# A graph layer on one core: the places of four pairs in one copy, a row of places in PSUM, two more gather buffers and narrower last blocks

## The chip, the core and the metric

The kernel runs on one core of a Trainium2 chip. A core has a matrix engine (PE, TensorE, with its weight loads counted apart as PEld), a vector engine (DVE), a scalar engine (ACT), a general engine (POOL, GpSimd), which here does nothing but gather rows by index, and SyncE (SP), which issues the plain copies from and to device memory. Working data lie in SBUF (128 partitions); PE writes to PSUM, eight banks of 512 f32 columns per partition. Each engine takes its instructions in order, and semaphores tie the engines together.

The metric is the device time of one launch in microseconds (us). The kernel before took 3597.59 us, the median of three runs from 3594.44 to 3604.85.

## What is computed

A message-passing layer over 12,500 nodes and 400,000 edges, with a GRU at the nodes. Edges come sorted by `dst`.

```
h   = max(layernorm(x), 0)
m   = relu(concat(h[src], h[dst], ea) @ w1 + b1) @ w2 + b2      # per edge, ea has 32 features
agg = segment_sum(m, dst)
gi, gh = agg @ w_ih + b_ih, h @ w_hh + b_hh
r, z = sigmoid(i_r + h_r), sigmoid(i_z + h_z);  n = tanh(i_n + r * h_n)
out = x + (1 - z) * n + z * h
```

## The kernel before

**Preparation.** The nodes are normalised in batches; `hT_all` keeps h transposed in SBUF, and the table A = h @ w1[0:128] goes to device memory. Then small tables are made on DVE (lines 349 to 391): the first node of each pair (`base_f`), per block its first node (`blk_f`), the offsets of its pairs (`off_f`, `off_i`) and the step from the block before (`step_f`, `step_i`).

**The loop over edges.** 128 edges make a tile, 8 tiles a *pair* k (391 of them), half a pair a *unit* u (782). In one pair all edges go to two windows of 32 nodes each, since `dst` is sorted. Per pair:

- `gather` (line 136): eight indirect copies on POOL bring the rows A[src] of 128 edges each into a G buffer (a few first pairs take x instead). G buffers come from a pool of `GBUFS` and, at first, another of `EARLY`.
- `fetch_d` (486) and `fetch` (478): on SP's queue the places (`dst`, broadcast to 32 partitions, one copy for each half, into a tile Ld) and the edge features (into partitions 64 to 95 of a tile L), for QP = 2 pairs at a time.
- `onehot_T` (496): DVE compares Ld with the node numbers and writes the transposed one-hots into partitions 0 to 63 of L.
- `window_copy`, `window_product`, `window_rows` (506, 522, 529): the 64 columns of h of the two windows times w1[128:256], written with the bias into RW.
- `pre` (593): PE multiplies L with RW, which adds the window's row and the feature part. `add` (616): DVE adds G. `relu` (628): ACT writes RB.
- `onehot` (537): DVE compares each edge's place in its window (`dloc`, f16) with the row 0 to 31 (`iota`, f16 in SBUF). `seg` (636): PE sums RB over the edges of a window into a PSUM bank; `take` (649) copies the sums out.

`stages(u)` runs these as a pipeline: one-hots three pairs ahead, `pre` three units ahead, `add` and `relu` two units ahead, `seg` of the unit itself.

**By hand.** 43 of the 391 pairs are not gathered by POOL: their columns of h are copied one at a time, by ACT (line 789, 19 pairs) and DVE (796 and 801, 24 pairs), spread over the loop from u = 2 * JOBS0 on, where JOBS0 = 2 * EARLY + GBUFS.

**The nodes.** Every 14 pairs make a block of 512 nodes. `node(b)` (657) is a generator: it adds up the pairs' sums (PE, lines 674 to 682), carries the overlap of the block before (`carry`), makes four gates (`gate`, each of products with `brow`, `whh_s`, `w2ih`), the elementwise work and the transposes back, and stores. The loop runs one step of it per unit, in phase 3 of `other`. The last block (13 pairs) runs as a whole behind the loop.

PSUM holds two banks each for `oh` (window products, and the transposes of the preparation), `pre` and `seg`, and one each for `nd` and `misc`. `check_windows` sets a flag when the windows don't hold all edges, and a slow general path would follow; for these inputs it isn't taken.

Of the kernel before, what the change touches and what calls it, by code (L numbers as in the profile page):

```python
# [28 lines left out]
V = 32  # L29
# [4 lines left out]
NB = -(-NP // BP)  # L34
DMIN = 320
QP = 2
# [5 lines left out]
GBUFS = 7  # L42
# [13 lines left out]
def tile_gnn(ctx: ExitStack, tc: tile.TileContext, x, src, srcT, dstT, dstP, eaT, eaP, w1, b1, w2T, b2,  # L56
# [12 lines left out]
    ps1 = ctx.enter_context(tc.tile_pool(name="ps1", bufs=1, space=bass.MemoryType.PSUM))  # L69
    dram = ctx.enter_context(tc.tile_pool(name="dram", bufs=1, space=bass.MemoryType.DRAM))  # L70
# [138 lines left out]
    with tc.tile_pool(name="pp", bufs=3) as pp:  # L209
# [76 lines left out]
        for q in range(NC + 3):  # L286
            if q < NC:
                b, i0, c, e, P, n0 = chunk(q)
                if c == 0:
                    stat(b + 2)  # L290
                    fin(b + 1)
            if 1 <= q <= NC:
                b, i0, c, e, P, n0 = chunk(q - 1)
                pts[q - 1] = ps2.tile([128, 512], F32, name="oh")
# [40 lines left out]

    p3 = ctx.enter_context(tc.tile_pool(name="p3", bufs=3, reuse_waits="tile"))
# [31 lines left out]
    nc.vector.tensor_scalar(blk_f, base_f[:, ::BP], float(N - BW), None, op0=ALU.min)  # L368
# [8 lines left out]
    for k0, k1, b0, b1_, n in ((0, (NB - 1) * BP, 0, NB - 1, BP),  # L377
                               ((NB - 1) * BP, NP, NB - 1, NB, NP - (NB - 1) * BP)):
        nc.vector.tensor_tensor(
            off_f[:, b0:b1_, :n], base_f[:, k0:k1].rearrange("o (b n) -> o b n", n=n),  # L380
            blk_f[:, b0:b1_, None].to_broadcast([1, b1_ - b0, n]), op=ALU.subtract)
        nc.vector.tensor_copy(base_i[:, b0:b1_, :n],
                              base_f[:, k0:k1].rearrange("o (b n) -> o b n", n=n))
    nc.vector.tensor_scalar(off_i, off_f, float(BW - V - SHIFT), 0.0, op0=ALU.min, op1=ALU.max)
# [3 lines left out]
    step_c = const.tile([1, NB], F32, name="step_c")  # L388
    nc.vector.tensor_scalar(step_c, step_f, float(BW), float(DMIN), op0=ALU.min, op1=ALU.max)
# [60 lines left out]
    def check_windows():  # L450
# [8 lines left out]
        pm = ps2.tile([128, 512], F32, name="oh")  # L459
# [3 lines left out]
        nc.vector.tensor_reduce(f[:, 6:7], off_f, AX.XY, ALU.max)  # L463
        nc.vector.tensor_reduce(f[:, 7:8], off_f, AX.XY, ALU.min)
        nc.vector.tensor_scalar(f[:, 1:2], f[:, 6:7], float(BW - V - SHIFT), None, op0=ALU.is_gt)
        nc.vector.tensor_scalar(f[:, 5:6], f[:, 7:8], 0.0, None, op0=ALU.is_lt)
        nc.vector.tensor_reduce(f[:, 2:3], step_f, AX.X, ALU.max)
        nc.vector.tensor_scalar(f[:, 3:4], blk_f[:, NB - 1:NB], float(N - BW), None,
                                op0=ALU.not_equal)
        nc.vector.tensor_copy(f[:, 4:5], f[:, 5:6])  # L470
        nc.vector.tensor_reduce(f[:, 6:7], f[:, 0:6], AX.X, ALU.max)
# [3 lines left out]
    Ls, Ds, OH, RT, HE, SEG = ({} for _ in range(6))  # L475
# [10 lines left out]
    def fetch_d(q):  # L486
        if q * QP >= NP:
            return
        n = min(QP, NP - q * QP)
        c = slice(q * QP * 512, (q * QP + n) * 512)  # L490
        Ds[q] = p3.tile([2 * V, QP * 512], I32, name="Ld")
        for a in range(2):
            nc.sync.dma_start(Ds[q][V * a:V * (a + 1), :n * 512],
                              dstP[a:a + 1, c].to_broadcast([V, n * 512]))

    def onehot_T(k):
        if k >= NP:
            return
        c = slice((k % QP) * 512, (k % QP + 1) * 512)
        nc.vector.tensor_scalar(Ls[k // QP][:2 * V, c], Ds[k // QP][:, c], node_of[:, k:k + 1],  # L500
                                None, op0=ALU.is_equal)
# [3 lines left out]

    def window_copy(k):
        if k >= NP:
            return
        b = k // BP
        if k % BP == 0:  # L510
            n = min(BP, NP - k)
# [25 lines left out]
    def onehot(k):  # L537
# [3 lines left out]
        OH[k] = OHB[k % len(OHB)]  # L541
        for a in range(2) if k == 0 else (None,):
            if a is None:
# [3 lines left out]
                i = iota[:, None, None, :]  # L547
            else:
# [3 lines left out]
                i = iota[:, None, :]  # L552
# [96 lines left out]
    def take(k):  # L649
        if k < 0:  # L650
            return
        pm = SEG.pop(k)
        nc.vector.tensor_copy(sums[:, k % BP, :], pm[:2 * V, :D])  # L653
        nc.scalar.copy(dcol[:2 * V, NP - 1 - k:NP - k], pm[:2 * V, D:D + 1])  # L654


    def node(b):

        def carry(o, p, d):
            m = BW - DMIN  # L660
# [4 lines left out]
        g0 = nc.sync.value_load(blk_i[0:1, b:b + 1], min_val=0, max_val=N - BW)  # L665
        xb = p3.tile([128, 4, D], F32, name="xb", bufs=1)
        nc.sync.dma_start(xb, x[bass.ds(g0, BW), :].rearrange("(p i) f -> p i f", i=4))
        n = min(BP, NP - b * BP)
        _, offs = nc.values_load_multi_w_load_instructions(
            off_i[0:1, b, 0:n], engines=[ET.PE], min_val=0, max_val=BW - V - SHIFT,  # L670
            skip_runtime_bounds_check_because="clamped above")
        pt = ps1.tile([128, 512], F32, name="nd")
        pd = ps1.tile([128, 512], F32, name="misc")
        nc.tensor.matmul(pt, zrow[:, :128], zrow, start=True, stop=False)
# [3 lines left out]
        nc.tensor.matmul(pd, zrow[:, :128], zrow, start=True, stop=False)  # L678
        for i in range(n):
            c = NP - 1 - (b * BP + i)  # L680
            nc.tensor.matmul(pd[:, bass.ds(offs[i], V + SHIFT)], dcol[:, c:c + 128], spot_h,
                             start=False, stop=i == n - 1)
        d = nc.vector.value_load(step_i[0:1, b:b + 1], min_val=DMIN, max_val=BW)
# [4 lines left out]
        g = nc.tensor.value_load(blk_i[0:1, b:b + 1], min_val=0, max_val=N - BW)  # L688
        hT = hT_all[:, bass.ds(g, BW)]

        def gate(name, i, with_h, with_s):
            c = slice(i * D, (i + 1) * D)
            ci = slice(2 * D, 3 * D) if i == 3 else c
            pg = ps1.tile([128, 512], F32, name=name)
            nc.tensor.matmul(pg, brow[:, c], DEG[:, :BW], start=True, stop=False)  # L695
            if with_h:
                nc.tensor.matmul(pg, whh_s[:, ci], hT, start=False, stop=not with_s)  # L697
            if with_s:
                nc.tensor.matmul(pg, w2ih[:, ci], TOT[:, :BW], start=False, stop=True)  # L699
            return pg  # L700

        def temp():
            return p3.tile([128, BW], F32, name="gt", bufs=3)
# [18 lines left out]
        gv = nc.vector.value_load(blk_i[0:1, b:b + 1], min_val=0, max_val=N - BW)  # L722
        q = r
        nc.vector.tensor_tensor(q, hT_all[:, bass.ds(gv, BW)], t, op=ALU.subtract)
# [5 lines left out]
        po = ps1.tile([128, 512], F32, name="nd")  # L730
# [5 lines left out]
        nc.sync.dma_start(out[bass.ds(g0, BW), :].rearrange("(p i) f -> p i f", i=4), xb)  # L736
# [109 lines left out]
    for q in range(2):  # L846
        fetch_d(q)
        fetch(q)
    fetch_d(2)
# [38 lines left out]

    for u in range(NU):
        k, h = divmod(u, 2)  # L890
        gathers(u)
        if h == 0:
            if k % QP == 0:
                fetch_d(k // QP + 3)
                fetch(k // QP + 2)
            if k % BP == 0 and k:
                nodes_left.append([node(k // BP - 1), 2])
# [12 lines left out]
        def other(phase):  # L910
# [9 lines left out]
            if phase == 3:  # L920
# [183 lines left out]
```

## Time and profile before

| | before |
|---|---|
| median of three runs | 3597.59 us (3594.44 to 3604.85) |
| the profiled execution: its time / its span | 3598.83 us / 3597.1 us |
| busy: PE, DVE, ACT, POOL | 74%, 68%, 70%, 75% of the span |
| mean granted TensorE clock | 0.778 |
| gathers on POOL: count, mean | 2704 from A at 969 ns, 77 from x at 948 ns |
| copies on SP's queue for dst / for features | 392 / 196 |

A row of the page's groups reads: line, engine, operation, tile written <- tiles read, shapes, count | busy us, mean ns of one | idle time of the engine just ahead of them, and what ended most of it. "issue" there is idle time in which the engine waited for nothing that the profile shows. Rows of waits read: engine, tile and line that waited <- who ended the wait: us in total, times, longest. Rows of the timeline and of the chain begin with the start in us from the span's start and the length in us. The span is the time from the first to the last instruction; a run's time lies a little above it.

### The profile page before, as it was taken

What the parts mean: (1) busy time and instruction counts of PE and PEld (TensorE: products, weight loads), DVE (VectorE), ACT (ScalarE), POOL (GpSimd) and SP (SyncE); (2) the same over time, 40 slices, a digit from 0 to 9 for tenths busy, and PEclk for the clock granted to TensorE, in tenths of its full rate; (3) what the DMA queues carried; (4) which work ended last, traced back from release to release, by engine and by line L of the source; (5) the groups of instructions that cost most, each with busy time, mean ns of one, the idle gap of its engine ahead of it and who ended that gap; (6) DMA issues with size and microseconds to landing.
All of it is one profiled execution on the core that took longest, in us unless ns stands there. A gap on an engine that the chain in (4) does not pass through costs nothing. (4 is left out here: it accounts for less than half of the span.)

```text
span 3597.1 us, 76803 instructions
## 1 busy us (share of the span) xinstructions
PE 2664.4 (74%) x13674; PEld 1618.5 (45%) x13674; DVE 2445.7 (68%) x16547; ACT 2506.7 (70%) x20936; POOL 2694.2 (75%) x2789
## 2 busy tenths in 40 slices
PE   7697677677767776876777777677767776776876
PEld 6454344444434443443444444444444443443443
DVE  8766667677667667667666677676667677766652
ACT  5445567777777777777777777777777677767771
POOL 7677777777777777777777777777777777777774
PEclk9787888787877877777786888787777778786777
DMA  6333333333333333333333333333333333333331
GB/s 207 86 100 87 86 88 88 92 86 89 87 88 85 87 89 85 89 86 89 86 86 89 86 88 88 92 87 88 88 87 86 85 89 84 89 85 87 81 86 41
DMA packets 145458, 321.60 MB, mean 89 GB/s; under 512 B 58913, under 2 KB 64844, under 8 KB 144967
## 3 DMA queue, kind: packets, MB, share of 16 engines
q0 software_dynamic: 88992, 182.43, 20.7%
q1 hardware_dynamic: 55831, 134.16, 13.5%
q14 instruction: 379, 3.10, 0.3%
q8 instruction: 112, 1.84, 0.2%
q10 hardware_dynamic: 144, 0.07, 0.0%
HBM read 302.60 MB, written 13.84 MB: 88 GB/s over the span
## 5 line engine op out<-in xcount | busy, mean ns | idle before, releaser
L145 POOL DMA_INDIRECT G<-A,src_i x2704 | 2620.3, 969 | 835.3 <-issue 780.1
L789 ACT COPY HE_act<-hT_all 128x4 uint8 x19456 | 1983.0, 189 | 585.6 <-issue 583.7
L796 DVE SCALAR_TENSOR_TENSOR both<-hT_all 128x4 uint16 x12288 | 1097.0, 155 | 954.0 <-issue 947.2
L601 PE MATMUL pre<-RW,L 128*128 128x256 f32 x3128 | 1171.0, 503 | 730.5 <-DVE G L626 633.8
L601 PEld LDWEIGHTS pre<-RW,L 128*128 128x128 f32 x3128 | 677.1, 241 | 1068.8 <-DVE G L626 811.0
L632 ACT ACTIVATE RB<-G 128x512 f32<-128x512 f32 x676 | 424.5, 628 | 353.5 <-issue 143.4
L645 PE MATMUL seg<-RB,OH 128*32 128x129 f32 x6250 | 642.8, 340 | 4.3 <-ACT dcol L654 4.3
L626 DVE TENSOR_TENSOR G<-pre,G 128x512 f32<-128x512 f32 x676 | 462.5, 684 | 64.1 <-DMA G<-A,src_i 41.7
L645 PEld LDWEIGHTS seg<-RB,OH 128*32 128x32 f32 x6250 | 349.5, 130 | 232.2 <-issue 127.9
L526 PE MATMUL oh<-w1b,hw 128*64 128x128 f32 x782 | 213.0, 364 | 123.8 <-DVE hw L519 120.4
L535 DVE TENSOR_TENSOR RW<-oh,b1b 32x128 f32<-32x128 f32 x782 | 217.2, 278 | 11.5 <-PE oh L526 6.2
L526 PEld LDWEIGHTS oh<-w1b,hw 128*64 128x64 f32 x782 | 91.6, 166 | 294.2 <-DVE hw L519 210.6
L500 DVE TENSOR_SCALAR L<-Ld,node_of 64x512 f32<-64x512 int32 x391 | 192.2, 492 | 0.7 <-issue 0.6
L553 DVE TENSOR_TENSOR OH<-dloc,iota 128x256 f32<-128x256 f16 (+1 forms) x392 | 161.0, 411 | 0.2
L676 PE MATMUL nd<-spot,sums 64*128 64x40 f32 x782 | 116.9, 319 | 0.0
L676 PEld LDWEIGHTS nd<-spot,sums 64*128 64x128 f32 x782 | 113.0, 229 | 7.9 <-issue 7.9
L653 DVE COPY sums<-seg 64x128 f32<-64x128 f32 x391 | 107.1, 274 | 4.9 <-PE seg L645 3.7
L640 PE MATMUL seg<-zrow 1*64 1x129 bf16 x391 | 106.4, 272 | 3.0 <-ACT dcol L654 3.0
L519 DVE COPY hw<-hT_all 128x64 f32 x391 | 87.6, 224 | 24.6 <-issue 23.4
L801 DVE COPY HE_dve<-both 128x512 uint8<-128x512 uint8 x192 | 88.0, 458 | 6.6
L145 POOL DMA_INDIRECT G<-in_x,src_i x77 | 73.0, 948 | 25.1 <-issue 22.9
L640 PEld LDWEIGHTS <-zrow 1*64 1x64 bf16 x391 | 43.4, 111 | 94.7 <-issue 94.7
(148 smaller groups left out, 1605.0 us busy)
## 6 DMA issues: line engine op xcount, KB each, us to landing
Ld<-in_dstP SPq DMA_DIRECT2D x390, 128.0 KB
L<-in_eaP SPq DMA_DIRECT2D x195, 256.0 KB
G<-A,src_i POOLq DMA_INDIRECT x2704
xb<-in_x SPq DMA_DIRECT2D x28, 256.0 KB
out<-xb SPq DMA_DIRECT2D x28, 256.0 KB
xs<-in_x SPq DMA_DIRECT2D x11, 512.0 KB
A<-asb SPq DMA_DIRECT2D x11, 512.0 KB
src_i<-in_srcT SPq DMA_DIRECT2D x19, 80.0 KB
```

The costliest lines, as they stand in the source:

```text
L145: nc.gpsimd.indirect_dma_start(out=G[k][:, j, a, :], out_offset=None, in_=table, in_offset=bass.IndirectOffsetOnAxis(ap=src_i[c][:, i:i + ...
L500: nc.vector.tensor_scalar(Ls[k // QP][:2 * V, c], Ds[k // QP][:, c], node_of[:, k:k + 1], None, op0=ALU.is_equal)
L526: nc.tensor.matmul(PB_[k][:2 * V, :D], HW.pop(k).rearrange("p a v -> p (a v)"), w1b, start=True, stop=True)
L535: nc.vector.tensor_tensor(RW[k % 4][s, a, :], pm[s, :D], b1b[s, :], op=ALU.add)
L553: nc.vector.tensor_tensor(o, d.to_broadcast(shape), i.to_broadcast(shape), op=ALU.is_equal)
L601: nc.tensor.matmul(PP[u][:, 2 * i:2 * i + 2, :], Ls[k // QP][:, c0:c0 + 128], RW[k % 4], start=True, stop=not raw)
L626: nc.vector.tensor_tensor(RT[u], PP.pop(u), RT[u], op=ALU.add)
L632: nc.scalar.activation(o[:, :, :D], RT.pop(u), AF.Relu)
L645: nc.tensor.matmul(SEG[k][V * a:V * (a + 1), :D + 1], OH[k][:, j, a, :], RB[u % 3][:, (j % 2) * 2 + a, :D + 1], start=False, stop=all(b != ...
L676: nc.tensor.matmul(pt[:, bass.ds(offs[i], V + SHIFT)], sums[:, i, :], spot, start=False, stop=i == n - 1)
L789: nc.scalar.copy(he[:, e * 4:e * 4 + 4], column(v))
L796: nc.vector.scalar_tensor_tensor(both[:, (e0 % PIECE + i) // 2, :], column(vals[i + 1]), 256.0, column(vals[i]), op0=ALU.mult, op1=ALU.add)
```

## The change

The change does these things at once:

- **Copies.** QP goes from 2 to 4, Ld and `fetch_d` go. One copy brings the places of both halves of four pairs, broadcast to 64 partitions, straight into partitions 0 to 63 of L, and a second the features. `onehot_T` works in place. L has 2 buffers in place of 3. The copies of a group are issued where the last pair of the group two before it begins (k % 4 == 3).
- **Row of places.** The two `oh` banks become two fixed tiles `wide`; columns 128 to 159 of each hold a copy of `iota` as f32, and `onehot` reads it from the bank that the next window product doesn't write.
- **G buffers.** GBUFS goes from 7 to 9; JOBS0, and with it the start of the columns by hand, moves from 15 to 17 pairs.
- **Blocks.** `BLOCKS` lists the blocks: 26 of 14 pairs and 512 nodes as before, then 12 pairs (512 nodes), 7 (320), 6 (256) and 2 (128). The tables are made in five groups. `node` works on the block's width. A node starts behind `take` in phase 3; from pair 376 on it runs two steps a unit, from pair 389 on four.

```diff
+BLOCKS = [(BP * b, BP, BW) for b in range(26)] + [(364, 12, BW), (376, 7, 320), (383, 6, 256), (389, 2, 128)]
+NB = len(BLOCKS)
+NW = 27
+LEAST = [DMIN] * (NW + 1) + [192, 128]
+QP = 4
-GBUFS = 7
+GBUFS = 9
...
+    wide = [ps1.tile([128, 512], F32, name=f"wide{i}") for i in range(2)]
...
+    for w in wide:
+        nc.vector.tensor_copy(w[:, D:D + V], iota)
...
+    groups = [(0, NW - 1, 0, BP, BW)] + [(b, b + 1) + BLOCKS[b] for b in range(NW - 1, NB)]
+    for b0, b1_, k0, n, w in groups:
+        nc.vector.tensor_scalar(blk_f[:, b0:b1_], base_f[:, k0:k0 + (b1_ - b0 - 1) * n + 1:n], float(N - w),
+                                None, op0=ALU.min)
...
+    for b0, b1_, k0, n, w in groups:
+        ks = base_f[:, k0:k0 + (b1_ - b0) * n].rearrange("o (b n) -> o b n", n=n)
+        nc.vector.tensor_tensor(off_f[:, b0:b1_, :n], ks,
+                                blk_f[:, b0:b1_, None].to_broadcast([1, b1_ - b0, n]), op=ALU.subtract)
+        nc.vector.tensor_copy(base_i[:, b0:b1_, :n], ks)
+        nc.vector.tensor_scalar(off_c[:, b0:b1_, :n], off_f[:, b0:b1_, :n], float(w - V - SHIFT), 0.0,
+                                op0=ALU.min, op1=ALU.max)
+        nc.vector.tensor_scalar(step_c[:, b0:b1_], step_f[:, b0:b1_], float(BLOCKS[max(b0 - 1, 0)][2]),
+                                float(LEAST[b0]), op0=ALU.min, op1=ALU.max)
...
-        Ls[q] = p3.tile([128, QP * 512], F32, name="L")
+        Ls[q] = p3.tile([128, QP * 512], F32, name="L", bufs=2)
+        p = dstP[:, c]
+        nc.sync.dma_start(
+            Ls[q].bitcast(I32)[:2 * V, :n * 512],
+            bass.AP(tensor=p.tensor, offset=p.offset, ap=[list(p.ap[0]), [0, V], [1, n * 512]]))
         nc.sync.dma_start(Ls[q][2 * V:, :n * 512], eaP[:, c])
...
-        nc.vector.tensor_scalar(Ls[k // QP][:2 * V, c], Ds[k // QP][:, c], node_of[:, k:k + 1],
-                                None, op0=ALU.is_equal)
+        nc.vector.tensor_scalar(Ls[k // QP][:2 * V, c], Ls[k // QP].bitcast(I32)[:2 * V, c],
+                                node_of[:, k:k + 1], None, op0=ALU.is_equal)
...
-        PB_[k] = ps2.tile([128, 512], F32, name="oh")
+        PB_[k] = wide[k % 2]
...
+        row = wide[(k + 1) % 2][:, D:D + V]
...
-                i = iota[:, None, None, :]
+                i = row[:, None, None, :]
...
+            m = before - LEAST[b]
             nc.vector.tensor_tensor(o[:, 0:m], p[:, 0:m], o[:, bass.ds(d, m)] if b else
                                     o[:, BW:BW + m], op=ALU.add)
-            nc.vector.tensor_copy(o[:, m:BW], p[:, m:BW])
+            if m < w:
+                nc.vector.tensor_copy(o[:, m:w], p[:, m:w])
+            if w < before:
+                nc.vector.memset(o[:, w:before], 0.0)
...
+    def steps(k, phase):
+        hurry = 1 if k < BLOCKS[NW][0] else 2 if k < BLOCKS[-1][0] else 4
+        return phase >= 4 - hurry
...
-            if k % QP == 0:
-                fetch_d(k // QP + 3)
+            if k % QP == QP - 1:
                 fetch(k // QP + 2)
-            if k % BP == 0 and k:
-                nodes_left.append([node(k // BP - 1), 2])
...
-            if phase == 3:
+                if k and k == BLOCKS[block(k)][0]:
+                    for it, _ in nodes_left:
+                        run(it)
+                    nodes_left[:] = [[node(block(k) - 1), 1 if k > BLOCKS[NW][0] else 2]]
+            for _ in range(steps(k, phase)):
                 step(nodes_left)
```

In `check_windows` the two long reductions of `off_f` and three small operations become one reduction of the marks that the tables now hold.

More of the change, by code (lines that the diff above doesn't have):

```diff
@@ L376, in tile_gnn @@
     nc.vector.memset(off_f, 0.0)
[L377 to L384, printed above, removed]
+    off_c = const.tile([1, NB, 16], F32, name="off_c")
+    nc.vector.memset(off_c, 0.0)
+    step_c = const.tile([1, NB], F32, name="step_c")
     nc.vector.tensor_tensor(step_f[:, 1:], blk_f[:, 1:], blk_f[:, :-1], op=ALU.subtract)
     nc.vector.memset(step_f[:, 0:1], float(BW))
-    step_c = const.tile([1, NB], F32, name="step_c")
-    nc.vector.tensor_scalar(step_c, step_f, float(BW), float(DMIN), op0=ALU.min, op1=ALU.max)
+    for b0, b1_, k0, n, w in groups:
[7 more added lines that the diff above has]
+                                float(LEAST[b0]), op0=ALU.min, op1=ALU.max)
+    nc.vector.tensor_copy(off_i, off_c)
+    nc.vector.tensor_tensor(off_f, off_f, off_c, op=ALU.not_equal)
     nc.vector.tensor_copy(step_i, step_c)
@@ L462, in check_windows @@
         nc.vector.tensor_reduce(f[:, 0:1], pm[0:1, :128], AX.X, ALU.max)
[L463 to L466, printed above, removed]
+        nc.vector.tensor_reduce(f[:, 1:2], off_f, AX.XY, ALU.max)
         nc.vector.tensor_reduce(f[:, 2:3], step_f, AX.X, ALU.max)
-        nc.vector.tensor_scalar(f[:, 3:4], blk_f[:, NB - 1:NB], float(N - BW), None,
+        nc.vector.tensor_scalar(f[:, 3:4], blk_f[:, NB - 1:NB], float(N - BLOCKS[-1][2]), None,
                                 op0=ALU.not_equal)
-        nc.vector.tensor_copy(f[:, 4:5], f[:, 5:6])
-        nc.vector.tensor_reduce(f[:, 6:7], f[:, 0:6], AX.X, ALU.max)
+        nc.vector.tensor_reduce(f[:, 6:7], f[:, 0:4], AX.X, ALU.max)
         nc.vector.tensor_copy(flag, f[:, 6:7])
-    Ls, Ds, OH, RT, HE, SEG = ({} for _ in range(6))
+    Ls, OH, RT, HE, SEG = ({} for _ in range(5))
     hand = {}
@@ L551, in onehot @@
                 shape = [128, e - a * GRP, V]
-                i = iota[:, None, :]
+                i = row[:, None, :]
             nc.vector.tensor_tensor(o, d.to_broadcast(shape), i.to_broadcast(shape),
@@ L677, in node @@
                              start=False, stop=i == n - 1)
-        nc.tensor.matmul(pd, zrow[:, :128], zrow, start=True, stop=False)
+        nc.tensor.matmul(pd, zrow[:, :128], zrow[:, :w], start=True, stop=False)
         for i in range(n):
-            c = NP - 1 - (b * BP + i)
+            c = NP - 1 - (k0 + i)
             nc.tensor.matmul(pd[:, bass.ds(offs[i], V + SHIFT)], dcol[:, c:c + 128], spot_h,
                              start=False, stop=i == n - 1)
-        d = nc.vector.value_load(step_i[0:1, b:b + 1], min_val=DMIN, max_val=BW)
+        d = nc.vector.value_load(step_i[0:1, b:b + 1], min_val=LEAST[b], max_val=before)
         yield 1
@@ L693, in gate @@
             ci = slice(2 * D, 3 * D) if i == 3 else c
-            pg = ps1.tile([128, 512], F32, name=name)
-            nc.tensor.matmul(pg, brow[:, c], DEG[:, :BW], start=True, stop=False)
+            pg = ps1.tile([128, 512], F32, name=name)[:, :w]
+            nc.tensor.matmul(pg, brow[:, c], DEG[:, :w], start=True, stop=False)
             if with_h:
@@ L698, in gate @@
             if with_s:
-                nc.tensor.matmul(pg, w2ih[:, ci], TOT[:, :BW], start=False, stop=True)
+                nc.tensor.matmul(pg, w2ih[:, ci], TOT[:, :w], start=False, stop=True)
             return pg
         def temp():
-            return p3.tile([128, BW], F32, name="gt", bufs=3)
+            return p3.tile([128, BW], F32, name="gt", bufs=3)[:, :w]
         pr = gate("nd", 0, True, True)
@@ L729, in node @@
         yield 1
-        po = ps1.tile([128, 512], F32, name="nd")
+        po = ps1.tile([128, 512], F32, name="nd")[:w // 4, :]
         for i in range(4):
@@ L846, in tile_gnn @@
     for q in range(2):
-        fetch_d(q)
         fetch(q)
-    fetch_d(2)
     for k in range(3):
```

54 lines of the change are left out of this document (22 added, 32 removed).

## The prediction

> **What bounds the kernel now.** I read the page first, then the waits of POOL, the waits of DVE by stretches, and last the end of the run.
>
> ```profile
> span 3597.1 us, 76803 instructions
> PE 2664.4 (74%) x13674; PEld 1618.5 (45%) x13674; DVE 2445.7 (68%) x16547; ACT 2506.7 (70%) x20936; POOL 2694.2 (75%) x2789
> L145 POOL DMA_INDIRECT G<-A,src_i x2704 | 2620.3, 969 | 835.3 <-issue 780.1
> ...
> POOL G L145 <- issue: 803.0, 2635, 0.3
> ...
> POOL G L145 <- PE misc L586: 11.6, 1, 11.6
> ...
> L145 POOL DMA_INDIRECT G<-A,src_i x2704: 940/944/2132, 99.9 to 3554.4; - x194
> ```
>
> No engine is over 75% busy, yet POOL never rests: between two gathers lie 0.3 us of issue, and only once in the whole run, for 11.6 us, does it wait for anybody. From 99.9 to 3554.4 us it issues 2704 gathers, (3554.4 - 99.9 - 11.6) / 2703 = 1.274 us apart. A gather takes 944 ns at the median, 969 on the mean: 2704 x 25 ns = 68 us are delays.
>
> ```profile
> DVE both L796 <- issue: 622.5, 515, 2.5
> DVE hw L519 <- issue: 14.5, 18, 1.1
> ...
> L553 DVE TENSOR_TENSOR OH<-dloc,iota 128x256 f32<-128x256 f16 x240 | 98.8, 412 | 0.0
> ...
> DVE G L626 <- DMA G<-A,src_i: 14.5, 13, 2.4
> ...
> DVE G L626 <- DMA G<-A,src_i: 22.9, 6, 4.3
> ...
> DVE G L626 <- DMA G<-A,src_i: 4.2, 1, 4.2
> ```
>
> These are DVE's waits from 264 to 2400 us (first two rows, with L553 of the same stretch), from 2400 to 3400, from 3400 to 3557 and behind. Up to 2400 DVE waits for nothing but its own register loads: it is full, at 2136 / 240 = 8.9 us a pair, 4.45 us a unit. From 2400 on it catches up with POOL and waits 14.5 us for gathers; at the very end 22.9 + 4.2 = 27.1 us more. So two engines are at parity: POOL made faster by itself gives DVE back 14.5 + 27.1 = 41.6 us and not one more.
>
> ```profile
> 3485.00:3513.00 28.00, 26.70 (x150) 15.74 (x150) 14.66 (x37) 23.46 (x204) 21.44 (x22) 1.00 0.32 84
> 3513.00:3526.00 13.00, 13.00 (x101) 8.73 (x95) 6.75 (x18) 4.39 (x13) 9.95 (x11) 1.00 0.37 102
> 3526.00:3557.00 31.00, 13.52 (x84) 7.95 (x82) 6.56 (x16) 3.91 (x9) 22.34 (x24) 0.86 0.21 54
> ...
> 3557.00:3597.10 40.10, 29.05 (x73) 12.94 (x73) 6.97 (x13) 2.65 (x6) 0.00 (x0) 0.50 0.02 8
> ...
> 3557.11 0.70 DVE G L626
> ...
> 3560.42 5.70 PE nd L676 x26
> ...
> 3568.25 2.04 PE nd L695 x2
> ...
> 3587.77 0.61 ACT gt L720
> ...
> 3591.03 0.69 DVE xb L734
> ```
>
> The windows show length, then busy time of PE, its loads, DVE, ACT, POOL, and the granted clock. The hand-made columns end here, and PE is full (26.7 of 28 us, then 13.0 of 13.0) at clock 1.00. Then everything waits for gathers, PE falls to 13.5 of 31 us, and the tail behind the last add (3557.11 to 3597.1, 40 us) runs at a granted 0.50. The chain of waits names its parts: sums of 13 pairs 5.7 us, gates 19.5 us (3568.25 to 3587.77).
>
> **The parts: more G buffers, 7 to 9.** Pair 11 now waits 11.6 us for the buffer of pair 0. With two more buffers pairs 11 and 12 (16 gathers, 20 us) are gathered meanwhile, so the wait goes whole: POOL -11.6 us.
>
> **The row of places in PSUM.**
>
> ```profile
> 1011.15 0.42 DVE L553 TENSOR_TENSOR OH<-dloc,iota 128x256 f32<-128x256 f16 x1
> 1011.20 1.19 POOL L145 DMA_INDIRECT G<-A,src_i  x1 [0.30 <-issue]
> ...
> 1026.40 0.69 DVE L626 TENSOR_TENSOR G<-pre,G 128x512 f32<-128x512 f32 x1
> 1026.43 0.95 POOL L145 DMA_INDIRECT G<-A,src_i  x1 [0.30 <-issue]
> ...
> L712 DVE TENSOR_TENSOR gt<-gt,misc 128x512 f32<-128x512 f32 x28 | 19.2, 687 | 14.6 <-PE misc L697 11.1 <-ACT gt L708 2.8
> L726 DVE TENSOR_TENSOR gt<-gt 128x512 f32<-128x512 f32 x28 | 19.0, 680 | 4.3 <-ACT gt L720 4.3
> ```
>
> L553 reads two SBUF tensors; the gather started inside it takes 1.19 us instead of 0.944, that is, something it needs 0.12 us after its start waits until 1011.57, where L553 ends. L626 reads one tensor from PSUM and one from SBUF, covers that same moment, and the gather takes 0.95. The change makes L553 of L626's kind. A one-hot of 412 ns meets that moment in 412 / 1274 of the cases and then delays by 206 ns: 391 x 0.0666 = 26 us of POOL's 68. I take -26 (bounds 0 and -26). On DVE the operand costs what L712 against L726 costs, 7 ns, 391 times 0 to 3 us: 0.
>
> [...]
>
> **One copy for the places of 4 pairs, one-hots in place.** 588 issues on SP become 196. SP is a bystander:
>
> ```profile
> SPq L493 <- DVE L L500: 2920.5, 191, 25.2
> q1 hardware_dynamic: 55831, 134.16, 13.5%
> q0 software_dynamic: 88992, 182.43, 20.7%
> ...
> 205.26 0.69 DVE L626 TENSOR_TENSOR G<-pre,G 128x512 f32<-128x512 f32 x1 [0.37 <-PE pre L601]
> ...
> 209.04 0.69 DVE L626 TENSOR_TENSOR G<-pre,G 128x512 f32<-128x512 f32 x1 [0.37 <-PE pre L601]
> ```
>
> It waits 2920 us for buffers, so fewer issues cost and give 0. The bytes stay the same. What changes is the time allowed: the L tile of a group comes free with the last product of the group two before, and its first one-hot stands 6 units later, 26.7 us at 4.45 us a unit. Queue q1 keeps 16 rings busy 13.5% of the span, 7770 us for 134.16 MB, so 17.3 GB/s a ring: 512 KB take 1.9 us on sixteen rings. The new pattern has the two rows of dstP outermost; if that leaves it two rings, 15.2 us, and 15.2 / (1 - 0.207) = 19.2 beside the gathers. Both fit in 26.7. They don't fit where units are short: around pairs 16 to 23, without jobs, two units take 3.78 us (205.26 to 209.04), six 11.3. Two groups there wait 2 x 0 to 2 x 8 us; I take 5, since the pattern speaks for two rings.
>
> **The prologue and the flags.**
>
> ```profile
> 99.79 0.84 DVE L365 TENSOR_SCALAR node_of<-base_b,place_c 32x391 f32<-32x391 f32 x2 [13.13 <-POOL place_c L360]
> ...
> 101.26 0.43 DVE L376 MEMSET off_f<- 1x448 f32 x1
> ...
> 102.65 0.15 DVE L379 TENSOR_TENSOR off_f<-base_f,blk_f 1x13 f32<-1x13 f32 x1
> ```
>
> The two copies of the row stand ahead of a 13 us wait and are covered by it; without that wait they cost 0.4 us. Behind it stand 4 more pieces of blk_f and 14 more of the five groups (18 x 0.15 = 2.7 us), a memset (0.43), a cast and a comparison over 480 elements (0.9): 4 us on DVE, which is the path. check_windows loses a long reduction and three small ones: -1. Together +3.
>
> **Narrower blocks.** Blocks 26 to 29 hold 12, 7, 6, 2 pairs instead of 14 and 13. Node 26 is now stepped twice a unit while DVE is full. In the end stretch of before, such steps made DVE wait
>
> ```profile
> DVE gt L712 <- ACT gt L708: 2.8, 1, 2.8
> ...
> DVE gt L715 <- PE nd L699: 1.8, 1, 1.8
> ...
> 3484.70 1.12 PE L695 MATMUL nd<-DEG,brow 33*128 33x512 f32 x2
> ...
> 3517.87 0.63 PE L645 MATMUL seg<-RB,OH 128*32 128x129 f32 x8
> ...
> 3521.65 0.63 PE L645 MATMUL seg<-RB,OH 128*32 128x129 f32 x8
> ```
>
> 4.6 us: 0 to 6, I take +3. Node 27 and the first steps of node 28 fall where PE is full. At clock 1.00 a gate instruction over 512 columns takes 0.53 us (L695, two in 1.12 with overlapping ends), so 0.33 over 320: 20 of them 6.6, 14 sums at 0.2, zeroing and transposes 1.4: 10.8 us. Node 28 gives 12 sums, zeroing and the first gate: 4.7. Together +15.5 (bounds 0, where gathers are still awaited, and 15.5; PE full says 15.5). A plain unit takes PE (3521.65 - 3517.87) / 2 = 1.9 us there.
>
> The last add: -14.5 - 27.1 + 3 + 5 + 3 + 15.5 = -15.1, from 3557.1 to 3542. POOL, earlier by 11.6 + 26 = 37.6, lets it.
>
> The tail: behind the last add now stand the rest of node 28 (256 columns), with the last three seg products between its steps, and then node 29 (128 columns, 2 pairs). Halving L712's 687 ns for 256 columns gives 0.4 per step: add and relu 1.4, eight such steps 3.2, one gate that nothing hides 1.6, transposes, xb and seg 1.9: 8. Node 29: sums 1.4, carry 1.0, gates 20 x 0.15 = 3.0, elementwise 1.5, transposes and xb 1.3: 8.2. From xb's end to the span's end 3597.1 - 3591.7 = 5.4. Sum 21.6 at clock 1.00; if PE's 8 us take twice as long at 0.50, 29.6. I take 24, since PE comes in full: 3542 + 24 = 3566, 31 us under the span of 3597.1. The profiled execution's own time is 3598.8, 1.2 above the median of the three: 3567.8, and for the median 3566.5.
>
> **The rivals.**
>
> POOL remains the bound (0.17): PE finds room for nodes 27 and 28 and no copy is late. Then the last add goes the whole 37.6 us: 3519.5 + 24 = 3543.5, a time of 3545. For it: 13.5 of 31 us busy on PE in the last window. Against: the full PE before it.
>
> The row doesn't do what it says (0.16): the gathers stay at 969, POOL gives 11.6 alone. Last add 3545.5, PE rests again, tail 29: 3574.5, a time of 3575. Against: the four rows above.
>
> The copy on two rings is late (0.12), the slower side: one-hot L500 then waits in every group of DVE's full stretch. It decides from 26.7 us to landing, 1.4 times the 19.2 above; every us beyond costs 96 groups a us each. At 28 us: 1.3 x 96 = 125, less the 31 gained: some 3690. For it: the gathers need the same rings. Against: L500 has 7 us of room. [...]
>
> Something uncounted takes the gain (0.05).
>
> **How the numbers follow.** Forecast 0.50, rivals 0.17, 0.16, 0.12, rest 0.05. Within 0.3% (11 us, about what this kernel's runs can tell apart) falls the rest and a little of the third: 0.06. Slower 0.12. Faster 0.82. The time is 3566; the range goes from the first rival, 3543, to 3593, which holds the second with a late copy of 18 us, and leaves the third out.
>
> **What would show it.** Right: gathers at a mean near 959 ns, none delayed at L553; no wait of POOL for L586; L626 waiting for gathers under 15 us in all; gates of the last node near 0.15 to 0.28 us; a tail under 30 us. Wrong: L500 waiting for a DMA hundreds of times; POOL still at 969; L553 over 430 ns; PE idle in the last 40 us ahead of the tail.

## The result and the profile after

The changed kernel takes 3589.6 us (median of six runs, 3582.9 to 3592.6) against 3602.2 for the kernel before (six runs, 3594.4 to 3605.9): a ratio of 0.9965, 95% interval 0.9954 to 0.9976. It is faster, by 12.5 us, where 31 were forecast. The profiled execution is the quickest of the six: its time is 3582.9 us, its span 3581.0. Line numbers are 2 to 10 higher than before, and the one-hot L500 is now L502, L553 is L559, L626 is L632.

The page and its groups, to be read against the first rows of the prediction:

```profile
span 3581.0 us, 76155 instructions
L149 POOL DMA_INDIRECT G<-A,src_i x2704 | 2602.1, 962 | 831.8 <-issue 780.6
L502 DVE TENSOR_SCALAR L<-L,node_of 64x512 f32<-64x512 int32 x391 | 191.4, 490 | 18.9 <-DMA L<-in_dstP 18.7
L559 DVE TENSOR_TENSOR OH<-dloc,wide 128x256 f32<-128x256 f16 (+1 forms) x392 | 159.6, 407 | 0.4 <-issue 0.4
q1 hardware_dynamic: 35803, 134.33, 13.9%
```

The gathers fell from 969 to 962 ns, the one-hot that reads the row didn't get slower (L559 407 ns, before 412), and a wait for the places has appeared, 18.7 us. DVE's waits by the stretches of the prediction (150 to 264, 2400 to 3400, 3400 to 3540, behind 3540; each row: who waited <- for whom: us, times, longest):

```profile
DVE L L502 <- DMA L<-in_dstP: 18.7, 2, 11.7
...
DVE G L632 <- PE pre L607: 0.4, 1, 0.4
...
DVE gt L722 <- PE misc L707: 8.9, 2, 5.6
DVE TOT L669 <- PE nd L686: 7.8, 2, 5.8
DVE G L632 <- PE pre L607: 7.2, 3, 5.7
...
DVE gt L722 <- PE misc L707: 8.1, 2, 5.1
DVE gt L725 <- PE nd L709: 3.9, 2, 2.8
```

No stretch has a row of L632 waiting for a gather any more: the 14.5 and 27.1 us of before are gone. At the end DVE waits for PE in their place.

The windows of the end, with the columns of the prediction's:

```profile
3485.00:3520.00 35.00, 28.65 (x155) 20.26 (x155) 14.63 (x54) 23.80 (x205) 26.69 (x28) 0.70 0.34 86
3520.00:3545.00 25.00, 25.00 (x155) 15.56 (x153) 14.31 (x37) 7.28 (x17) 10.72 (x12) 0.99 0.18 47
3545.00:3566.00 21.00, 20.00 (x100) 11.37 (x96) 5.43 (x17) 3.16 (x8) 0.00 (x0) 0.67 0.00 1
...
3551.40:3581.00 29.60, 22.95 (x81) 13.25 (x81) 6.87 (x21) 2.87 (x9) 0.00 (x0) 0.56 0.04 10
```

PE has hardly any rest from 3520 to 3566 (busy for 25.00 of 25 us, then 20.00 of 21), and just when the last products are left, its granted clock drops to 0.56. The timeline of that tail (start, length, engine, line; the wait ahead of it in brackets):

```profile
3550.42 0.29 DVE L669 TENSOR_TENSOR TOT<-nd,TOT 128x128 f32<-128x128 f32 x1 [3.15 <-PE nd L686]
...
3551.56 0.62 DVE L632 TENSOR_TENSOR G<-pre,G 128x512 f32<-128x512 f32 x1
...
3551.70 1.19 PE L705 MATMUL nd<-DEG,brow 33*128 33x256 f32 x2 [0.86 <-DVE DEG L674]
...
3557.30 0.42 DVE L722 TENSOR_TENSOR gt<-gt,misc 128x256 f32<-128x256 f32 x1 [5.13 <-PE misc L707]
...
3566.45 0.57 SPq L746 DMA_DIRECT2D out<-xb  x1
...
3577.25 0.35 SPq L746 DMA_DIRECT2D out<-xb  x1
```

The last add starts at 3551.56 (before 3557.11, forecast 3542). Behind it lie 29.5 us (before 39.9, forecast 24): 14.9 for the rest of node 28, 10.8 for node 29, 3.8 behind the last issue. Two gate instructions over 256 columns take 1.19 us, longer than the 1.12 that two over 512 took at clock 1.00.

Where the time went, from the two traces: the end of relu in after, less its end in before, at some units of the 782.

| unit | 0 | 20 | 28 | 540 | 700 | 752 | 758 | 776 | 781 | end of span |
|---|---|---|---|---|---|---|---|---|---|---|
| after less before, us | +2.5 | +8.7 | +19.6 | +15.1 | -3.6 | -10.1 | +0.3 | +7.2 | -5.6 | -16.1 |

17 us are lost between units 0 and 28, 4 won from there to 540, 25 between 540 and 752, 10 lost while node 26 runs, 7 while PE is full, 13 won at the end of the gathers, 10.5 in the tail.

### The profile page after: what moved, and what is told of

Read it like the earlier page. It is cut to its first block, busy times and chain, and to the rows that moved or that the text cites. A ratio compares the mean times of both kernels' runs of the same rounds, so it can differ in the third digit from the quotient of the medians.

```text
span 3581.0 us, 76155 instructions
## 1 busy us (share of the span) xinstructions
PE 2666.4 (74%) x13726; PEld 1624.9 (45%) x13726; DVE 2444.3 (68%) x16590; ACT 2504.8 (70%) x20942; POOL 2676.1 (75%) x2789
## 5 line engine op out<-in xcount | busy, mean ns | idle before, releaser
L651 PE MATMUL seg<-RB,OH 128*32 128x129 f32 x6250 | 635.3, 337 | 0.0
L632 DVE TENSOR_TENSOR G<-pre,G 128x512 f32<-128x512 f32 x676 | 462.9, 685 | 26.9 <-PE pre L607 17.2
L531 PE MATMUL wide<-w1b,hw 128*64 128x128 f32 x782 | 212.4, 363 | 133.0 <-DVE hw L524 129.4
L531 PEld LDWEIGHTS wide<-w1b,hw 128*64 128x64 f32 x782 | 91.1, 165 | 303.7 <-DVE hw L524 223.3
L540 DVE TENSOR_TENSOR RW<-wide,b1b 32x128 f32<-32x128 f32 x782 | 216.7, 277 | 13.3 <-PE wide L531 8.0
L502 DVE TENSOR_SCALAR L<-L,node_of 64x512 f32<-64x512 int32 x391 | 191.4, 490 | 18.9 <-DMA L<-in_dstP 18.7
L559 DVE TENSOR_TENSOR OH<-dloc,wide 128x256 f32<-128x256 f16 (+1 forms) x392 | 159.6, 407 | 0.4 <-issue 0.4
L705 PE MATMUL nd<-DEG,brow 33*128 33x512 f32 (+3 forms) x120 | 70.6, 671 | 28.2 <-ACT gt L718 17.3
```

The source lines that it names most:

```text
L502: nc.vector.tensor_scalar(Ls[k // QP][:2 * V, c], Ls[k // QP].bitcast(I32)[:2 * V, c], node_of[:, k:k + 1], None, op0=ALU.is_equal)
L531: nc.tensor.matmul(PB_[k][:2 * V, :D], HW.pop(k).rearrange("p a v -> p (a v)"), w1b, start=True, stop=True)
L540: nc.vector.tensor_tensor(RW[k % 4][s, a, :], pm[s, :D], b1b[s, :], op=ALU.add)
L559: nc.vector.tensor_tensor(o, d.to_broadcast(shape), i.to_broadcast(shape), op=ALU.is_equal)
L632: nc.vector.tensor_tensor(RT[u], PP.pop(u), RT[u], op=ALU.add)
L651: nc.tensor.matmul(SEG[k][V * a:V * (a + 1), :D + 1], OH[k][:, j, a, :], RB[u % 3][:, (j % 2) * 2 + a, :D + 1], start=False, stop=all(b != ...
```

## The experiments

Each kernel is compared with the kernel before, measured beside it. The table turns each ratio into us of 3602; single edits of it are told apart below. A difference of two of its rows carries the errors of both, some 6 to 8 us. Lengths and leads "by the traces" are those of one profiled run of each kernel.

| kernel | ratio, 95% interval | against before, us |
|---|---|---|
| the change | 0.9965 [0.9954, 0.9976] | -12.5 |
| x1: places by two copies | 0.9899 [0.9885, 0.9914] | -36 |
| x2: row read from SBUF | 1.0039 [1.0024, 1.0054] | +14 |
| x3: 7 G buffers | 1.0001 [0.9989, 1.0013] | 0 |
| x4: old blocks | 0.9918 [0.9905, 0.9931] | -30 |
| v1: node 26 one step a unit | 0.9941 [0.9927, 0.9954] | -21 |
| y1: x1's copies, node 26 one step a unit | 0.9878 [0.9864, 0.9893] | -44 |
| y2: x1's copies, old blocks | 0.9893 [0.9877, 0.9909] | -39 |
| v2: x1's copies, 7 G buffers | 0.9936 [0.9922, 0.9949] | -23 |
| v3: x1's copies, row from SBUF | 0.9992 [0.9981, 1.0003] | -3 |
| y3: before, with the row in PSUM alone | 0.9917 [0.9904, 0.9930] | -30 |
| y4: before, with the narrow blocks alone | 1.0011 [1.0002, 1.0020] | +4 |

**The copy of the places.** The theory: its pattern has the two halves outermost, which makes it slow, and that is what L502 waits for. That it moves on two rings, and x1's two copies on sixteen, as the expectations and the runs' names have it, was the author's assumption; the views show the share of the DMA engines and no count of rings.

```diff
-        p = dstP[:, c]
-        nc.sync.dma_start(
-            Ls[q].bitcast(I32)[:2 * V, :n * 512],
-            bass.AP(tensor=p.tensor, offset=p.offset, ap=[list(p.ap[0]), [0, V], [1, n * 512]]))
+        for a in range(2):
+            nc.sync.dma_start(Ls[q].bitcast(I32)[V * a:V * (a + 1), :n * 512],
+                              dstP[a:a + 1, c].to_broadcast([V, n * 512]))
```

> The changed kernel with the places of a group copied by two copies, one for each half, broadcast to 32 partitions each, instead of one whose outermost dimension is 2. Theory (the one copy runs on two rings, takes some 20 us and makes DVE wait twice for it around pairs 14 to 20, 18.7 us): both waits of the one-hot for the places go, DVE is that much earlier from pair 14 to pair 370, and the end is earlier by 10 to 13 us, where POOL's last gather (lands at about 3537 us) stops the gain: ratio to the kernel before 0.993. Rival (the waits early in the run are made up later, since POOL sets the end): ratio as the changed kernel's, 0.9965, and DVE waits for gathers instead.

In the change, the timeline shows the issue on SP and the one-hot that waits for it:

```profile
180.63 0.56 SPq L493 DMA_DIRECT2D L<-in_dstP  x1
...
207.48 0.56 SPq L493 DMA_DIRECT2D L<-in_dstP  x1
...
201.91 0.62 DVE L502 TENSOR_SCALAR L<-L,node_of 64x512 f32<-64x512 int32 x1 [7.07 <-DMA L<-in_dstP]
...
228.12 0.48 DVE L502 TENSOR_SCALAR L<-L,node_of 64x512 f32<-64x512 int32 x1 [11.67 <-DMA L<-in_dstP]
```

From issue to landing go 21.3 and 20.6 us for 512 KB. Meanwhile the DMA engines are far from full; the window from shortly after the first issue to the landing says so, and so do its first 7 us alone (the last two columns are the busy share of the sixteen DMA engines and GB/s):

```profile
183.00:190.00 7.00, 7.00 (x57) 5.86 (x57) 3.81 (x10) 3.31 (x8) 5.27 (x6) 1.00 0.55 136
183.00:201.90 18.90, 15.53 (x121) 11.88 (x120) 6.43 (x19) 4.55 (x11) 14.33 (x16) 1.00 0.40 102
```

The same group in x1, whose two copies have the 32 broadcast rows outermost, and its one-hot over the whole run:

```profile
183.00:190.00 7.00, 6.95 (x58) 5.56 (x59) 4.67 (x17) 4.21 (x12) 5.47 (x6) 1.00 0.96 209
...
L501 DVE TENSOR_SCALAR L<-L,node_of 64x512 f32<-64x512 int32 x391 | 192.1, 491 | 0.2
```

In the same 7 us the share is 0.96 at 209 GB/s in place of 0.55 at 136, and no wait of the one-hot is left. How many rings the one copy used is in no view; its 20.6 to 21.3 us lie near the 19.2 that the prediction worked out for an assumed two. The kernel goes from 0.9965 to 0.9899, 24 us, more than expected. By the traces x1 leads the change by 16 us at unit 28 and by 15 at the last: the loss arises in two groups and is never won back. The remaining 7 to 9 us lie between the profiled runs and the medians (the change's profiled run is 6.7 under its median, x1's 1.6 over its own).

**The row of places.** x2 and v3 read it from SBUF again, beside the one copy and beside x1's two; y3 puts it into PSUM in the kernel before, with nothing else of the change.

```diff
-        row = wide[(k + 1) % 2][:, D:D + V]
+        row = iota
```

> The changed kernel with the row of places read from SBUF again. Theory (the row in PSUM frees POOL of 26 us of delays, of which only what POOL would lack at the end counts): gathers at a mean of 969 to 971 ns instead of 962, last gather about 26 us later (3560 us), the end 10 to 15 us later: ratio 1.000. Rival (DVE is the bound to the end, POOL's pace doesn't matter any more): ratio 0.9965, gathers slower with no effect.

> The kernel before with one part of the change, the row of places in PSUM. Theory (26 us of delays go from POOL; the kernel before loses 41.6 us in DVE's waits for gathers, so they come back): gathers at 960 ns, last gather at about 3530 us, the end 20 to 26 us earlier: ratio 0.993 to 0.9945. Rival (DVE is the bound and the end hardly moves): ratio 0.998.

The gathers' groups of x2, of v3 and of y3:

```profile
L149 POOL DMA_INDIRECT G<-A,src_i x2704 | 2632.7, 974 | 835.0 <-issue 787.0
```

```profile
L149 POOL DMA_INDIRECT G<-A,src_i x2704 | 2634.5, 974 | 824.0 <-issue 784.2
```

```profile
L146 POOL DMA_INDIRECT G<-A,src_i x2704 | 2597.9, 961 | 835.3 <-issue 779.0
```

With the row in SBUF the mean is 974 ns in x2 and v3 and 969 in the kernel before; with it in PSUM it is 960 to 962. In busy time of POOL that makes 31 us (x2), 34 (v3) and 22 (y3). The row is worth 27 us (x2), 33 (v3) and 30 (y3) of the kernel's time. Both expectations above had the right sign and too small a size. In the change one sees it one gather at a time. The timeline shows the one-hot and the gather started 0.05 us into it:

```profile
3140.96 0.40 DVE L559 TENSOR_TENSOR OH<-dloc,wide 128x256 f32<-128x256 f16 x1
...
3141.01 0.94 POOL L149 DMA_INDIRECT G<-A,src_i  x1 [0.30 <-issue]
```

0.94 us, where the same meeting cost 1.19 before. Over the run, 115 gathers of the change have a one-hot at work 121 ns after their start; 112 of them take 960 ns at most. Before, 115 gathers ended their delay with a one-hot's end, 26.1 us together; in x2 and v3 it is 121 and 122 gathers and 32 us, in the change and in y3 none. The rival by which the row saves nothing would have 0 here; all three runs go against it.

y3 alone, at 0.9917, beats the whole change. Part of its 30 us is the tail: 22 are there at the last relu, the rest is a better clock (below).

**Two more G buffers.**

```diff
-GBUFS = 9
+GBUFS = 7
```

> The changed kernel with 7 G buffers. Theory (two more buffers save one wait of 11.6 us of POOL at 121 us, and POOL is 11 to 15 us ahead of need at the end): the wait is back, the end moves by 0 to 4 us: ratio 0.9965 to 0.9975. Rival (the buffers also let POOL run further ahead in the loop): more POOL waits along the run and over 8 us: ratio 0.999.

The theory fell: 13 us. The next guess was that the buffers matter because late copies let the gathers run dry, so v2 repeated it with x1's copies.

> On such a chip. Theory (the worth of the two G buffers hung on the late copies): 0.990 to 0.991 of before. Rival (13 us in every setting): 0.9935.

It fell too: 0.9936 against x1's 0.9899, 13 us again. POOL's waits in v2 name what the buffers take away:

```profile
POOL G L149 <- issue: 803.2, 2636, 0.3
...
POOL G L149 <- PE misc L591: 13.7, 1, 13.7
```

One wait of 13.7 us for the buffer of an early pair; the change has no such row. The sizes that both rivals gave came true, but how the wait would reach the end isn't shown: the further waits of POOL that x3's rival expects aren't there, and DVE waits for gathers 0 us in x3 and 1.2 in v2. The edit also does a second thing. JOBS0 contains GBUFS, so the columns by hand begin at pair 15 again instead of 17. DVE's gaps ahead of these columns are larger in x3 (first row) than in the change (second):

```profile
DVE both L806 <- issue: 948.7, 788, 2.5
```

```profile
DVE both L806 <- issue: 930.6, 793, 2.6
```

v2 against x1 gives 944.3 against 928.1. Leaving aside the six runs that could not tell (below), all five traces with 7 buffers have 944 to 962 us, all eight with 9 have 923 to 937. The loss may thus lie in the start of the columns and not in the buffers; no run parts the two. The size isn't firm either: v2's trace ends only 2.4 us behind x1's.

**The blocks.** x4 puts the 28 old blocks back with one step a unit; y4 brings the narrow ones into the kernel before; y2 is x4 with x1's copies.

```diff
-BLOCKS = [(BP * b, BP, BW) for b in range(26)] + [(364, 12, BW), (376, 7, 320), (383, 6, 256), (389, 2, 128)]
+BLOCKS = [(BP * b, BP, BW) for b in range(27)] + [(378, 13, BW)]
...
-        hurry = 1 if k < BLOCKS[NW][0] else 2 if k < BLOCKS[-1][0] else 4
-        return phase >= 4 - hurry
+        return phase >= 3
```

> The changed kernel with 28 blocks of 512 nodes as in the kernel before, stepped once a unit. Theory (the two steps a unit for node 26 cost 10 us, nodes 27 and 28 take PE just ahead of the end, and the tail gives back 10): no jump of 10 us at pairs 376 to 380, last add earlier and stopped by POOL's last gather at about 3538, tail 40 to 43 us: 3580 of span, ratio 0.996 to 0.998, so the narrow blocks are worth about nothing. Rival (narrow blocks are worth the shorter tail, 10 us or more): ratio 1.000.

> As the run with the copies on sixteen rings, with 28 blocks of 512 nodes, stepped once a unit. Theory (with the copies in time POOL's last gather sets the last add at about 3529 us, and the long tail of 43 us follows): span 3572, ratio 0.991 to 0.993, slightly worse than the narrow blocks with sixteen rings (0.9899). Rival (the narrow blocks cost 17 us wherever they stand, as the run with old blocks and two rings says): ratio 0.985.

> The kernel before with one part of the change, the narrower blocks and their steps. Theory (node 26's 10 us and node 27's PE work fill waits for gathers there, 27 us in all, so the shorter tail counts): last add about where it was, tail 33 instead of 43: ratio 0.997 to 0.998. Rival (the narrow blocks cost more than they give here too): ratio 1.002 or more.

The narrow blocks, meant here as the difference with and without them, cost 17 us beside the one copy (x4), 2 beside x1's two (y2 against x1) and 4 by themselves (y4). They gain nothing in any setting. None of the three ratios lies where its theory or its rival put it. The traces are steadier than the ratios. From unit 752 to the last relu the change and x1 take 119.6 us each, x4 98.6 and y2 99.4, so the blocks cost 20 to 21 us there in both settings, and a shorter tail gives a part back. In the kernel before the same stretch takes 115.1 us without them and 116.1 with them (y4). There DVE waits 27 us for gathers at the end, and y4's theory that the blocks fill such waits fits. That y4 still comes out slower arises ahead of the blocks: its trace is 17 us behind at unit 752, with 37.8 us of gathers delayed by one-hots against 26.1, and gains 9 from there to the end.

One reason for the cost was tested by itself: node 26 stepped once a unit, the doubled steps left to the later nodes.

```diff
-        hurry = 1 if k < BLOCKS[NW][0] else 2 if k < BLOCKS[-1][0] else 4
+        hurry = 1 if k < BLOCKS[NW + 1][0] else 2 if k < BLOCKS[-1][0] else 4
```

> As the run with the copies on sixteen rings, and node 26 stepped once a unit up to pair 382 instead of twice from pair 376. Theory (the two steps a unit put a gate of PE and its reader half a unit apart, so DVE and ACT wait for PE while both are full): the 10 us that the changed kernel loses against the kernel before between units 752 and 758 go, the last add comes 7 to 8 us earlier, where the last gather (lands about 3528 us) stops it, ratio 0.9875 against 0.9899. Rival (the loss is the node's work itself, moved to where both engines are full): ratio unchanged at 0.990, the loss spread over more units.

> On a chip on which the kernel before takes some 3600 us. Theory (node 26's double steps cost the same 8 us as with sixteen rings): 0.9943 of before. Rival (beside the late copies they cost 10 to 14 us): 0.992 to 0.993. On a chip like the last two this run says nothing.

Both are met: 8 us beside x1's copies, 9 beside the one. By the ratios alone this would not be clear, since the intervals of y1 and x1 overlap and those of v1 and the change touch. The traces show it at the place: from unit 752 to the last relu v1 takes 108.6 us and y1 109.6, where the change and x1 take 119.6. Two windows of equal length during node 26, first the whole stretch of the change in which the clock stands at 0.50, then one of v1:

```profile
3442.20:3459.30 17.10, 17.10 (x61) 9.87 (x59) 10.14 (x66) 9.15 (x81) 13.14 (x14) 0.50 0.23 60
```

```profile
3443.50:3460.60 17.10, 10.04 (x55) 5.73 (x55) 11.36 (x82) 12.70 (x112) 12.83 (x15) 0.80 0.29 82
```

With double steps PE is full for 17.1 us at a granted 0.50, and the columns on ACT fall back (81 instructions against 112). With single steps it has room at 0.80. x1 and y1 differ in the same way (PE busy for 17.10 of 17.10 us at 0.50, and for 14.52 at 0.70). y1 is the best version found, at 0.9878.

The other reason is the tail, which the narrow blocks shorten by less than they seem to. Windows of it in x4 and in y3, both with the old last block of 13 pairs:

```profile
3538.30:3577.40 39.10, 29.05 (x73) 12.94 (x73) 6.55 (x13) 2.65 (x6) 0.00 (x0) 0.51 0.02 8
```

```profile
3536.00:3567.20 31.20, 21.90 (x73) 11.25 (x73) 6.09 (x11) 2.23 (x6) 0.00 (x0) 0.66 0.03 10
```

The same 73 products take 39 us where the clock stays near 0.5, 31 where it comes back for a while. Why the clock differs isn't shown. Counted from the last add, the tails take 39.6 us in x4 and 32.4 in y3, and the change's 29.5 are a gain of 10 us or of 3.

**The row beside x1's copies.** v3 was to show whether part of the row's worth is hidden once the copies are in time.

> On such a chip. Theory (the row is worth 26 us in every setting): 0.9975 of before, mean gather near 970 ns. Rival (part of it is hidden once the copies are in time): 0.993 to 0.995.

0.9992 against x1's 0.9899: 33 us. Nothing is hidden; the row is worth a little more there than the theory said.

**Six runs that could not tell.** The kernels of v1, v2 and v3 were measured twice before, when the kernel before itself took 4946 and 4859 us.

> The changed kernel with its two-ring copy as it is, and node 26 stepped once a unit instead of twice; the doubled steps are left to node 27. Theory (the double steps of node 26 cost what they cost with sixteen rings, 0.9899 to 0.9878, some 8 us): 0.9943 of before. Rival (the double steps cost only where DVE already leads and is full, so that beside the late copies they are worth 10 to 14 us, and the narrow blocks of the change then fall to the old blocks' 0.9918): 0.992 to 0.993.

> The changed kernel with the copy of the places on sixteen rings and 7 G buffers instead of 9. Theory (the 13 us that two buffers were worth beside the two-ring copy came from the late copies: gathers ran dry while DVE waited for places; without late copies the two buffers are worth at most the one wait of POOL, which DVE as the bound hides): 0.990 to 0.991 of before, that is at most 4 us over the 0.9899 with 9 buffers. Rival (the two buffers are worth the wait itself, whatever the copies do): 0.9935, 13 us over.

> The changed kernel with the copy on sixteen rings and the row of places read from SBUF again. Theory (the row is worth the delays that it takes from the gathers, some 26 us, in every setting in which POOL is then near the bound): 0.9975 of before, with the gathers' mean back near 970 ns. Rival (with the copies in time DVE leads and part of the row's 26 us is hidden): 0.993 to 0.995.

> The same kernel as in the first try, whose chip took 4946 us for the kernel before and so could not tell. Theory (the double steps of node 26 cost what they cost with sixteen rings, 0.9899 to 0.9878, some 8 us): 0.9943 of before. Rival (beside the late copies they cost 10 to 14 us, and the narrow blocks of the change fall to the old blocks' 0.9918): 0.992 to 0.993.

> The changed kernel with the copy of the places on sixteen rings and 7 G buffers instead of 9, again. Theory (the 13 us that two buffers were worth beside the two-ring copy came with the late copies; without them DVE as the bound hides POOL's one wait): 0.990 to 0.991 of before. Rival (the two buffers are worth the wait itself, whatever the copies do): 0.9935.

> The changed kernel with the copy on sixteen rings and the row of places read from SBUF, again. Theory (the row is worth the delays that it takes from the gathers, some 26 us): 0.9975 of before, with the gathers' mean back near 970 ns. Rival (with the copies in time DVE leads and part of the row's 26 us is hidden): 0.993 to 0.995.

The ratios were 1.0051, 1.0027, 1.0038 and 1.0051, 0.9993, 1.0065. ACT's waits in z1, and in the change:

```profile
ACT HE_act L799 <- issue: 1655.2, 2421, 1.9
```

```profile
ACT HE_act L799 <- issue: 574.3, 598, 2.1
```

There ACT waits four times as often without anything that the profile shows. In z1's chain of the work that ended last, ACT's columns hold 22% of the span (2% in the change), and POOL waits 1287 us for ACT's relu, so what the disputed parts save is hidden. DVE's gaps grew too, from 931 to 1164 us. What slowed the issue isn't known; the later measurement, with 3597 us for the kernel before, gave the three v runs above.

## Why the prediction came out wrong in size

The direction was right, and 3589.6 lies in the range of 3543 to 3593. That is partly luck: the upper end stood for a row that saves nothing beside copies late by 18 us, and only the second of the two came. The gain was 12.5 us instead of 31. The two profiled runs differ by 16 us, and their stretches can be set against the terms of the forecast (by the ends of relu in the table above; the tail is what lies behind the last of them):

| stretch, term of the forecast | forecast, us | by the traces, us |
|---|---|---|
| to unit 0: prologue | +3 | +2.5 |
| units 0 to 28: late copies | +5 | +17.1 |
| units 28 to 540 | 0 | -4.5 |
| units 540 to 752: waits for gathers | -14.5 | -25.2 |
| units 752 to 758: node 26 | +3 | +10.4 |
| units 758 to 781: nodes 27 and 28, last waits for gathers | +15.5 - 27.1 | -5.9 |
| tail | -16 | -10.5 |
| sum | -31 | -16 |

By its own steps:

- **DVE's waits for gathers, -14.5 and -27.1: gone, but not worth what was forecast.** From unit 540 to 752 the change wins 25 us; y3 wins 23 in the same stretch, so most of it is the row's. DVE's gaps of issue there differ as well (263.1 us for 3456 copies before, 260.3 for 3576 after); why is open. Of the 27.1 at the end 17 came back even without the narrow blocks: that is what x4 wins on the kernel before from unit 758 to the last relu. POOL's last gather starts 21 us earlier (3533.1 against 3554.4), not 37.6, but the last add of the change doesn't wait for it.
- **Row in PSUM, -26 on POOL: right, in cause and size.** The delays that end with a one-hot, 26.1 us, are all gone. The three runs give 27, 30 and 33 us of the kernel's time. The rival at 3575, by which it would save nothing, falls.
- **G buffers, -11.6: POOL's wait is gone, as forecast.** The 13 us of the kernel's time in two settings are not explained by it (above).
- **Prologue, +3: right.** +2.5 at unit 0.
- **Late copies, +5: the first step that failed.** Its parts were at hand: 19.2 us, worked out for a copy on two rings, against 11.3 between issue and need. I took 5 out of 0 to 16, although I held the pattern to speak for two. That it leaves the copy two rings is shown by no run; in its place the runs showed a copy that was late. Measured: 18.7 us of waits (the copies took 21.3 and 20.6), 17 by the traces of before and after, 16 by x1's, 24 by the ratios. Where the length of a copy and its window are both worked out, the difference is the price. Elsewhere "both fit in 26.7" held: in the other 96 groups the one-hot never waits for its copy, so the slower rival has no place.
- **Node 26 stepped twice a unit, +3: the second.** 8 to 9 us by y1 and v1, 10 to 11 by their traces. I counted DVE's waits alone, 2.2 us in that stretch. The price sits on PE, which was filled (17.10 of 17.10 us) while its granted clock was 0.50, and on what ACT and DVE then did later.
- **Nodes 27 and 28 beside full PE, +15.5: too high.** From unit 758 to the last relu the narrow blocks cost 10 to 11 us (the change against x4, x1 against y2).
- **The tail, 24: the third.** It is 29.5. The prediction had 21.6 at clock 1.00 and 29.6 at half, and chose near the first "since PE comes in full". PE did come in full, and the clock was 0.56.

The single runs don't settle the sum. -30 (row, y3), -13 (buffers and start of the columns, x3 and v2), +4 (blocks, y4) and +24 (one copy in place of two, x1) make -15, near the -12.5 measured. With the values found in the change itself, -27 (x2) and +17 (x4), the sum is +1. The parts needn't add, each carries some 3 to 8 us, and the tail's clock alone moves a run by 8. This stays open.

## What to carry to other kernels

When several edits go in together, price each by the stage in which it can be late: a copy is judged in the shortest interval between its issue and its first use (here 11.3 us against 26.7 in DVE's full stretch, both worked out in the prediction), not in the mean one, and a loss on a full engine at 200 us can still be there at 3500 (x1's lead was 16 us at unit 28 and 15 at the last). Before copies are merged, see which dimension stands outermost (here 2 in place of 32 rows cost 24 us by the ratios). A change of one operand's place, from SBUF to PSUM, can be worth more than all that is built around it (y3's 30 us against 12.5 for the whole change), so it is tried alone first.

## What the runs showed of the hardware

- Two copies of 512 KB with two rows outermost took 21.3 and 20.6 us beside the gathers. From 2.4 us after the issue of the first to its landing the DMA share was 0.40 at 102 GB/s, in the first 7 us of that 0.55 at 136. In x1, with two copies of 256 KB and 32 rows outermost in each, the share in the same 7 us, from 0.8 us after the issue, reached 0.96 at 209 GB/s.
- The one-hot with both inputs in SBUF delayed a gather started inside it (1.19 us in place of 0.94); with one input in PSUM it didn't (0.94, and 112 of 115 such gathers took 960 ns at most). In the traces of before, x2, v3 and y4, with the row in SBUF, 115 to 128 of the 2704 gathers were delayed so, by 26 to 38 us together.
- PE, by its records busy for 17.10 of 17.10 us, had a granted clock of 0.50 throughout. Shortly behind 25 full us at 0.99, the last 29.6 us, with PE busy for 22.95 of them, had 0.56. The same tail of 73 products ran in 39.1 or 31.2 us, with the clock at 0.51 or 0.66.
- ACT's gaps of issue went from 574 us (the change; 575 in v1) to 1655 us (z1, v1's kernel measured at another time) for the same number of its column copies, and ACT's columns then held 22% of the chain that ended last, in place of 2%.
